# Two closings moved, one routing added: the end of a graph layer with a mixture of experts, replanned

## The chip, the cores and the metric

The kernel runs on one core of a Trainium2 chip. The metric is the device time of one execution in microseconds; three runs are given by their median. The core has five engines with a queue each: PE (matrix products), DVE and ACT (vector and scalar work), POOL (here it does nothing but issue indirect transfers: gathers and scatters of rows by a list of indices) and SP (it issues the plain transfers). Each queue is worked off in order. All transfers share 16 DMA engines.

## The reference

A layer on 6250 nodes of 256 numbers. The nodes are normalised; a graph convolution over 100,000 weighted edges and a linear attention are added; the sum is normalised again and goes through a mixture of 16 experts, of which each node takes two; a last normalisation and the sum are the output.

```python
xn = layernorm(x)
x = x + gnn(xn, edge_index, edge_weight) + mix(xn)       # graph convolution, linear attention
# L0_ffn on layernorm(x):
gate_logits = x @ gate_w + gate_b
topk_vals, topk_idx = top_k(gate_logits, 2)
topk_w = softmax(topk_vals)
h = relu(einsum('bsh,ehf->bsef', x, w1) + b1)            # 16 experts, 256 -> 512
expert_out = einsum('bsef,efh->bseh', h, w2) + b2        # 512 -> 256
y = x + sum over the two (topk_w * their expert_out)
out = old x + (y - mean(y)) / sqrt(var(y) + EPS) * gamma + beta
```

## The kernel before

The nodes lie in 49 tiles of 128 rows. The edges, sorted by their end node, lie in 782 chunks of 128. The kernel is one long hand-written order: a loop over slots, one chunk of edges in each slot, into which pieces of other work are woven. A piece is a generator that is put in at a slot and asks to be called again so many slots later. PE, DVE, ACT and SP execute what the loop writes, in its order. POOL's instructions are not held to that order: a scheduler places them, by what each depends on.

In each slot POOL gathers the 128 source rows of a chunk (`hrow`, L1479), DVE makes a 128 x 128 matrix of edge weights (`hot`, L1484) and PE adds their product into an accumulator (`acc`, L1492). Six to eleven slots lie between the gather of a chunk and its product. When the accumulator of a tile is whole, `residual` makes the tile's new rows, two tiles at a time, and the gate's logits.

After some tiles (`PHASES`, 8, 12, 16 and so on up to 49) a routing follows (`route`, some 70 small instructions on DVE): each of the new tiles' tokens gets two slots in a list of blocks of 128 tokens, each block belonging to one expert. `scatter` then writes the tokens' rows into the slots, two scatters of POOL for each tile (L1144). A block that isn't full stays open, and the next phase's tokens go on filling it. At one phase, the one after `CUT`, the open blocks are closed, so that from there on no token of the tiles below `CUT` stands in a block still to be computed. A closed block may have rows that no token uses.

`expert` computes one block: SP loads its weights (`w1`, `w2` with `b1` and `b2`, 1.15 MB in all) and its rows, PE transposes (L1215) and multiplies them (L1226, L1237), ACT applies the relu (L1233), and SP stores the result (`w_yslots`, issued at L1172). There are always 112 blocks. `hi` says up to which block number each phase's blocks may be begun, `block` at which slots: 7, 6, 5 or 4 slots apart.

`combine` finishes two tiles: POOL gathers each token's two result rows (L1283), DVE adds them, weighted, to the normalised row (L1299, L1301), ACT sums squares (L1306), DVE scales and adds (L1314 to L1320), SP stores the output row (L1321). Which blocks must have been stored before a tile's gather may start is in `LIMITS`: pairs of a tile and a number of blocks. The gather of a tile below 36 waits for block 84, one below 40 for block 99, one below 46 for block 108, the rest for all 112. These bounds depend on the data; `usual` keeps whether they held, and if they didn't, a second pass runs all experts again.

The gathered rows lie in places called `got`: ten rows of `late` and the ten rows of the ring that held the accumulators' sums. A place is taken at the gather and given back after its last reader.

Of the kernel before, what the change touches and what calls it, by code (L numbers as in the profile page):

```python
# [24 lines left out]
F32 = mybir.dt.float32  # L25
# [7 lines left out]
P = 128  # L33
N = 6250
D = 256
# [86 lines left out]

PHASES = (8, 12, 16, 20, 24, 28, 32, 36, 40, 46, NT)
CUT = 36
AFTER = PHASES.index(CUT) + 1
FIRST, USUAL = 2 * PHASES[AFTER] + 5, 2 * NT + 14
LIMITS = ((CUT, FIRST), (PHASES[AFTER], 2 * NT + 2), (PHASES[-2], 2 * NT + 11))
MOST = P  # L130

RING = 10
# [140 lines left out]
def windowed_layer(ctx: ExitStack, tc: tile.TileContext, X, x, ident, loc_t, w_t, src_t, src_r, zero_b, shared, W, b, gamma, beta, wqT, wkvT, wprojT, bproj,  # L273
# [897 lines left out]
    def sync(to, source):  # L1171
        issued[0] = nc.sync.dma_start(to, source).ins  # L1172
        return issued[0]
# [98 lines left out]
    def combine(ts_, homes, pool, last, ahead=9):  # L1272

        n, r = len(ts_), rows(ts_[0])
        total = pool.tile([P, 2], F32, name="total", bufs=3)[:r, :n]
        less = pool.tile([P, 2], F32, name="less", bufs=3)[:r, :n]
        squares = pool.tile([P, 2], F32, name="squares", bufs=3)[:r, :n]
        rs = pool.tile([P, 2], F32, name="rs", bufs=3)[:r, :n]
        got = {}
        for i, t in enumerate(ts_):  # L1280
            for k in range(2):
                got[i, k] = homes["got"].take()
                g = nc.gpsimd.indirect_dma_start(  # L1283
                    out=got[i, k]()[:r], out_offset=None, in_=yslots,
                    in_offset=IndirectOffsetOnAxis(ap=slot_i[:r, t, k:k + 1], axis=0)).ins
                m = next((m for m, (b, _) in enumerate(LIMITS) if t < b), None)
                if m is not None and LIMITS[m][1] - 1 in stores:
                    tc.declare_no_dep(g, group=f"late_{m}", reason="later blocks hold no token of the first tiles")
                    tc.add_manual_dep(g, stores[LIMITS[m][1] - 1].name, mybir.DependencyInfo(mybir.DependencyClass.Sync, mybir.DependencyReason.DATA), reason="the last of their blocks")
                    tc.add_to_no_dep_group(f"gathers_{m}", g)  # L1290
            yield 1
        yield ahead
        both = (pool if pool is not mp_main else xq).tile([P, 2, D], F32, name="xn2", bufs=3)[:r]
        for i, t in enumerate(ts_):
            act(both[:, i, :], X[:r, t, :], AF.Identity, bias=nm2[:r, t:t + 1], scale=rs2[:r, t:t + 1])
        yield 1
        for i, t in enumerate(ts_):
            y = both[:, i, :]
            v.scalar_tensor_tensor(y, got[i, 0]()[:r], w12[:r, t, 0:1], y, op0=OP.mult, op1=OP.add)  # L1299
            homes["got"].give(got[i, 0])  # L1300
            v.scalar_tensor_tensor(y, got[i, 1]()[:r], w12[:r, t, 1:2], y, op0=OP.mult, op1=OP.add,  # L1301
                                   accum_out=total[:, i:i + 1])
            yield 2 if i < n - 1 else 1
        act(less, total, AF.Identity, scale=-1.0 / D)
        for i in range(n):
            act(got[i, 1]()[:r], both[:, i, :], AF.Square, bias=less[:, i:i + 1], accum_out=squares[:, i:i + 1])  # L1306
            homes["got"].give(got[i, 1])
        sd = pool.tile([P, 2], F32, name="sd2", bufs=2)[:r, :n]
        act(sd, squares, AF.Sqrt, bias=eps_t[:r], scale=1.0 / D)
        yield 5  # L1310
        v.reciprocal(rs, sd)
        for i, t in enumerate(ts_):
            y = both[:, i, :]
            v.scalar_tensor_tensor(y, y, less[:, i:i + 1], last[:r, 0, :], op0=OP.add, op1=OP.mult)  # L1314
            o = pool.tile([P, D], F32, name="row", bufs=3)
            if t in shifted:
                v.scalar_tensor_tensor(o[:r], y, rs[:, i:i + 1], shifted[t]()[:r], op0=OP.mult, op1=OP.add)
            else:
                v.scalar_tensor_tensor(y, y, rs[:, i:i + 1], last[:r, 1, :], op0=OP.mult, op1=OP.add)
                v.tensor_add(o[:r], y, X[:r, t, :])  # L1320
            sync(out[t * P:t * P + r, :], o[:r])  # L1321
            yield 2


# [75 lines left out]
    for n, b in enumerate(PHASES):  # L1400
        flush = b == NT
        for t0 in range(a, b, 2):
            t1 = min(b, t0 + 2)
            lag = 3 if t0 < PHASES[AFTER] else 2 if t0 < PHASES[-2] else 1
            at = max(at, evicted_at(min(NCH, 16 * t1 + 4) - 1) - 1)
            weave.add(at, residual(range(t0, t1), lag, 2))
            if t0 >= QT:
                weave.add(at - 8, load_queries(range(t0, t1)))
            last_at = at
            for t in range(t0, t1):  # L1410
                summed_at[t] = at + 3
                if t + RING < NT and t >= 4:
                    sum_from(t + RING)
            at += 10
        hi = 2 * b - (9 if n < AFTER else -1 if n == AFTER else 4)
        ready = max(last_at + residual_slots(lag, 2) + 1, scattered - 2)
        more = min(lag, 3 if n < AFTER else 1)
        def routed(a=a, b=b, lo=lo, hi=hi, n=n, flush=flush, more=more):
            yield from route(a, b, lo, hi, n == 0, n == AFTER, more)
            if flush:  # L1420
                yield 1
                yield from close(hi, USUAL)
        weave.add(ready, routed())
        if flush or n == AFTER:
            weave.add(ready + 6, token_weights(*((CUT, NT) if flush else (0, CUT))))
        slow = 0 if flush else 1
        weave.add(ready + 2, scatter(n, a, b, 8 + more, "token" if slow else "got", slow))
        scattered = ready + 10 + more + 2 * (b - a) * slow
        ready += 13 + more + 2 * (b - a) * slow
        for j in range(lo, USUAL if flush else hi):  # L1430
            ends[j] = hi if j < hi else USUAL
            block = max(block + (4 if n > AFTER or block > NCH - 9 else 5 if n == AFTER else 6 if n == 5 or n == 6 else 7), ready)
            gap = (7, 0) if block < 16 * 30 else (6, 3)
            apart, behind = (5, 3) if block < 16 * 30 else (6, 3) if n < AFTER else (3, 1) if j == USUAL - 1 else (5, 2)
            weave.add(block, expert(n, j, homes, bank, gap, apart, behind, flush))
            stored_at[j] = block + sum(gap) + 2 * apart + behind + 4
        lo, a = hi, b
# [7 lines left out]
        yield  # L1445
    weave.add(last_at + residual_slots(lag, 2) + 1, load_last())
    weave.add(last_at + residual_slots(lag, 2) + 1 + 22, shift(range(NT - 16, NT), last))
    at = last_at + residual_slots(lag, 2) + 1
    for t0 in range(0, NT, 2):
        at = max(at, stored_at[min(block_of(t0), USUAL) - 1])  # L1450
        weave.add(at, combine(range(t0, min(NT, t0 + 2)), homes, mp, last))
# [59 lines left out]
    with tc.If(again[0]), ExitStack() as tail:  # L1511
        tail.enter_context(by_hand(tc))
        mp = tail.enter_context(tc.tile_pool(name="w_again", bufs=2))
        ps = tail.enter_context(tc.tile_pool(name="w_again_ps", bufs=8, space=bass.MemoryType.PSUM))
        last = mp.tile([P, 2, D], F32, name="last", bufs=1)
        nc.sync.dma_start(last[:, 0, :], bcast(f_gamma, D))
        nc.sync.dma_start(last[:, 1, :], bcast(f_beta, D))

        def places(n, size, name):
            tiles = [mp.tile([P, size], F32, name=f"{name}{j}", bufs=1) for j in range(n)]  # L1520
            return Places(*[((), lambda t=t: t) for t in tiles])

        homes = {"x": places(4, D, "x"), "xT": places(2, D, "xT"), "hT": places(2, F, "hT"),
                 "y": places(2, D, "y"), "w1": places(4, WA, "w1"), "w2": places(4, WROW - WA, "w2"), "got": places(8, D, "got")}
        weave = Weave()
        block = 0
        loaded.clear()
        stores.clear()
        shifted.clear()
        row = bank("row")  # L1530
        nc.tensor.matmul(row[0:1, :P], s["code"], ident, start=True, stop=True)
        listed(row, 0, MOST, True)
        for j in range(MOST):
            ends[j] = MOST
            weave.add(block, expert(None, j, homes, bank, (5, 4), 2, 1))
            block += 4
        block += 18
        for t0 in range(0, NT, 2):
            weave.add(block, combine(range(t0, min(NT, t0 + 2)), homes, mp, last, 3))
            block += 6  # L1540
        slot = 0
        while weave.steps:
            weave.run(slot)
            slot += 1
# [485 lines left out]
```

## Time and profile before

| what | value |
|---|---|
| three runs | 1403.89, 1403.41, 1399.54 us (median 1403.41) |
| the profiled execution | 1397.1 us |
| its span in the profile | 1395.2 us |
| mean granted clock of PE | 0.931 |
| PE busy | 1177.9 us, 84% of the span |
| PE's weight loads busy | 983.3 us, 70% |
| POOL busy | 968.4 us, 69% |
| DVE busy | 926.9 us, 66% |
| ACT busy | 523.1 us, 37% |
| moved by DMA | 349 MB, 250 GB/s over the span |

The span is what the profile of one execution covers; the profiled execution's own time is 1.9 us longer, and the median of the three runs lies above both. Busy shares are means over stages of quite different kinds, so they don't name what bounds the kernel; that has to be read stage by stage. POOL's queue holds 752 gathers of edge rows, 98 scatters and 98 gathers of result rows; SP's holds the loads and stores of the blocks and the output.

### The profile page before, as it was taken

How to read it: one execution, taken by the hardware profiler on the slowest of the kernel's cores; microseconds unless marked ns; L12 is line 12 of the kernel's file. 1: busy time of each engine (PE TensorE's matmuls, PEld its weight loads, DVE VectorE, ACT ScalarE, POOL GpSimd, SP SyncE). 2: the span in 40 equal slices, each digit the busy share in tenths (PEclk: the TensorE clock that was granted, in tenths of full speed). 3: DMA queues.
4: the chain of work that ended last, by engine and by line, in shares of the span. 5: the costliest groups of instructions: out<-in, count | busy, mean ns of one | idle time of the engine just before them, and what ended most of it. 6: DMA issues, size and time to landing. Idle time of an engine off the chain costs nothing. (4 is left out here: it accounts for less than half of the span.)

```text
span 1395.2 us, 24302 instructions
## 1 busy us (share of the span) xinstructions
PE 1177.9 (84%) x6908; PEld 983.3 (70%) x6908; DVE 926.9 (66%) x3215; ACT 523.1 (37%) x1476; POOL 968.4 (69%) x1009
## 2 busy tenths in 40 slices
PE   6989999988867589978798699798987998997760
PEld 5757777766656479867687598687876897886650
DVE  8965444457998676847568377485684567646676
ACT  7874444422213123212222132232322233467673
POOL 5637777777777777777777777777777773257753
PEclk9999999998888789989999899898999998999995
DMA  9967667776434658877777788787878987999983
GB/s 299 315 210 247 207 188 228 230 237 191 136 102 128 212 189 279 270 236 252 267 242 252 228 270 286 251 311 247 266 235 284 311 284 239 344 384 383 374 303 97
DMA packets 172870, 349.27 MB, mean 250 GB/s; under 512 B 26460, under 2 KB 112350, under 8 KB 172720
## 3 DMA queue, kind: packets, MB, share of 16 engines
q1 hardware_dynamic: 96376, 189.97, 38.8%
q0 software_dynamic: 47712, 128.17, 29.5%
q10 hardware_dynamic: 28632, 29.40, 6.4%
q8 instruction: 61, 1.00, 0.3%
q14 instruction: 89, 0.73, 0.2%
HBM read 271.62 MB, written 75.81 MB: 249 GB/s over the span
## 5 line engine op out<-in xcount | busy, mean ns | idle before, releaser
L1479 POOL DMA_INDIRECT hrow<-w_hs,src_t x752 | 728.1, 968 | 256.4 <-issue 84.7
L1492 PE MATMUL acc<-hrow,hot 128*128 128x256 f32 x1548 | 429.5, 399 | 75.4 <-DMA hrow<-w_hs,src_t 68.5
L1492 PEld LDWEIGHTS acc<-hrow,hot 128*128 128x128 f32 x1548 | 281.1, 198 | 140.9 <-issue 89.1
L1484 DVE TENSOR_SCALAR hot<-iota_g,loc_t,w_t 128x128 f32<-128x128 f32 x782 | 248.9, 356 | 46.4 <-PE acc L1492 45.1
L1233 ACT ACTIVATE hT<-hp,early 128x128 f32<-128x128 f32 x280 | 79.9, 368 | 234.0 <-PE hp L1226 170.0
L1237 PE MATMUL yp<-early,hT 128*128 128x256 f32 x560 | 138.9, 393 | 0.1
L1226 PE MATMUL hp<-Q,early 128*128 128x128 f32 x944 | 120.1, 282 | 12.1 <-ACT Q L1220 12.1
L1226 PEld LDWEIGHTS hp<-Q,early 128*128 128x128 f32 x944 | 118.1, 199 | 15.3 <-ACT Q L1220 12.8
L1237 PEld LDWEIGHTS yp<-early,hT 128*128 128x128 f32 x560 | 109.6, 199 | 16.5 <-ACT hT L1233 0.8
L1144 POOL DMA_INDIRECT w_xslots<-Q,slot_i x92 | 91.1, 990 | 30.6 <-issue 23.3
L1226 PEld LDWEIGHTS hp<-Q 128*128 128x128 f32 x848 | 104.6, 196 | 2.3
L1226 PE MATMUL hp<-Q 128*128 128x128 f32 x848 | 106.1, 279 | 0.0
L1233 ACT ACTIVATE hT<-hp,Q 128x128 f32<-128x128 f32 x168 | 48.0, 369 | 144.8 <-issue 110.0
L705 PE MATMUL kq<-early,xnT 128*128 128x512 f32 (+1 forms) x196 | 93.7, 601 | 5.2 <-ACT xnT L701 5.2
L713 DVE SCALAR_TENSOR_TENSOR row<-two_a,two_b 128x256 f32<-128x256 f32 (+1 forms) x49 | 20.8, 425 | 96.4 <-ACT two_b L710 96.4
L1237 PE MATMUL yp<-Q,hT 128*128 128x256 f32 x336 | 80.5, 383 | 0.0
L1283 POOL DMA_INDIRECT late<-w_yslots,slot_i x48 | 49.2, 1026 | 39.9 <-issue 22.3
L1237 PEld LDWEIGHTS yp<-Q,hT 128*128 128x128 f32 x336 | 62.8, 192 | 8.0
L350 ACT ACTIVATE sd<-mv,eps_t 128x2 f32<-128x2 f32 (+2 forms) x51 | 15.3, 300 | 127.1 <-DVE mv L346 117.3
L1247 DVE TENSOR_TENSOR Q<-yp,early 128x256 f32<-128x256 f32 x58 | 24.4, 421 | 56.4 <-PE yp L1237 55.8
L709 ACT ACTIVATE two_a<-kq 128x512 f32<-128x512 f32 (+1 forms) x49 | 29.3, 597 | 87.1 <-PE kq L705 66.8
L1215 PE MATMUL xtp<-ident,Q 128*128 128x128 f32 x224 | 43.6, 276 | 20.9 <-DMA Q<-w_xslots 20.6
(374 smaller groups left out, 1941.7 us busy)
## 6 DMA issues: line engine op xcount, KB each, us to landing
early<-in_experts SPq DMA_DIRECT2D x58, 642.0 KB
early<-in_experts SPq DMA_DIRECT2D x59, 512.0 KB
Q<-in_experts SPq DMA_DIRECT2D x53, 512.0 KB
Q<-in_experts SPq DMA_DIRECT2D x30, 642.0 KB
w_yslots<-zero_b ACTq DMA_DIRECT2D x16, 1024.0 KB
Q<-w_xslots SPq DMA_DIRECT2D x112, 128.0 KB
w_yslots<-Q SPq DMA_DIRECT2D x112, 128.0 KB
hrow<-w_hs,src_t POOLq DMA_INDIRECT x752
```

The lines of the kernel that those rows point to most:

```text
L705: nc.tensor.matmul(kq[:r], xnT[:, k, :r], wkq[:, k, :], start=(k == 0), stop=(k == 1))
L709: act(e[:r].rearrange("p a c -> p (a c)"), kq[:r], AF.Exp)
L1144: i = nc.gpsimd.indirect_dma_start(out=xslots, out_offset=IndirectOffsetOnAxis(ap=slot_i[:r, t, k:k + 1], axis=0), in_=y[:r], in_offset=No ...
L1215: nc.tensor.transpose(tp[:, c, :], xs[:, c * P:(c + 1) * P], ident)
L1226: nc.tensor.matmul(hp[:, f, :], w1[:, c, f * P:(f + 1) * P], xT[:, c, :], start=(c == 0), stop=(c == 1))
L1233: act(hT[:, f, :], hp[:, f, :], AF.Relu, bias=b1[:, f:f + 1], scale=1.0)
L1237: nc.tensor.matmul(yp[:, :D], hT[:, f, :], w2[:, f, :], start=(f == 0), stop=(f == FJ - 1 and not as_row))
L1247: v.tensor_add(y, yp[:, :D], b2)
L1283: g = nc.gpsimd.indirect_dma_start(out=got[i, k]()[:r], out_offset=None, in_=yslots, in_offset=IndirectOffsetOnAxis(ap=slot_i[:r, t, k:k + ...
L1479: nc.gpsimd.indirect_dma_start(out=hrows[c], out_offset=None, in_=hs, in_offset=IndirectOffsetOnAxis(ap=src_t[:, c:c + 1], axis=0))
L1484: v.tensor_scalar(hots[c], iota_g[:, group_of(c) % 2, :], loc_t[:, c:c + 1], w_t[:, c:c + 1], op0=OP.is_equal, op1=OP.mult)
L1492: nc.tensor.matmul(accs[g], hots.pop(c), hrows.pop(c), start=begin, stop=end)
```

## The change

The open blocks are closed at the routing after tile 28 (it was 36), a routing at tile 44 is added, and with them the limits, the pace of the blocks and the bounds `hi` are set anew: tiles below 28 wait for block 68, those below 32 for block 97, those below 40 for block 104, those below 46 for block 108. `LATER` is a new name for the phase at 40, from which lags and paces switch as before. The combines begin 13 slots later, counted from the last residual, so that in the written order they stand behind the last scatter. The output row is written into the place of the tile's second gathered row and no longer into one of three rows of its own; the place is given back after the store of the row instead of after ACT's sum of squares. (The second pass gets 14 such places instead of 8.)

```diff
-PHASES = (8, 12, 16, 20, 24, 28, 32, 36, 40, 46, NT)
-CUT = 36
+PHASES = (8, 12, 16, 20, 24, 28, 32, 36, 40, 44, 46, NT)
+CUT = 28
 AFTER = PHASES.index(CUT) + 1
 FIRST, USUAL = 2 * PHASES[AFTER] + 5, 2 * NT + 14
-LIMITS = ((CUT, FIRST), (PHASES[AFTER], 2 * NT + 2), (PHASES[-2], 2 * NT + 11))
+LIMITS = ((CUT, FIRST), (PHASES[AFTER], 2 * NT), (40, 2 * NT + 7), (PHASES[-2], 2 * NT + 11))
+LATER = PHASES.index(40)
...
             act(got[i, 1]()[:r], both[:, i, :], AF.Square, bias=less[:, i:i + 1], accum_out=squares[:, i:i + 1])
-            homes["got"].give(got[i, 1])
...
-            o = pool.tile([P, D], F32, name="row", bufs=3)
+            o = got[i, 1]()
             if t in shifted:
                 v.scalar_tensor_tensor(o[:r], y, rs[:, i:i + 1], shifted[t]()[:r], op0=OP.mult, op1=OP.add)
             else:
                 v.scalar_tensor_tensor(y, y, rs[:, i:i + 1], last[:r, 1, :], op0=OP.mult, op1=OP.add)
                 v.tensor_add(o[:r], y, X[:r, t, :])
             sync(out[t * P:t * P + r, :], o[:r])
+            homes["got"].give(got[i, 1])
...
-            lag = 3 if t0 < PHASES[AFTER] else 2 if t0 < PHASES[-2] else 1
+            lag = 3 if t0 < PHASES[LATER] else 2 if t0 < PHASES[-2] else 1
...
-        hi = 2 * b - (9 if n < AFTER else -1 if n == AFTER else 4)
+        hi = 2 * b - (9 if n < AFTER else 0 if n == AFTER else 5 if b == 44 else 4)
         ready = max(last_at + residual_slots(lag, 2) + 1, scattered - 2)
-        more = min(lag, 3 if n < AFTER else 1)
+        more = min(lag, 3 if n < LATER else 1)
...
-            block = max(block + (4 if n > AFTER or block > NCH - 9 else 5 if n == AFTER else 6 if n == 5 or n == 6 else 7), ready)
+            block = max(block + (4 if n > LATER or block > NCH - 9 else 6 if n > 3 else 7), ready)
             gap = (7, 0) if block < 16 * 30 else (6, 3)
-            apart, behind = (5, 3) if block < 16 * 30 else (6, 3) if n < AFTER else (3, 1) if j == USUAL - 1 else (5, 2)
+            apart, behind = (5, 3) if block < 16 * 30 else (6, 3) if n < LATER else (3, 1) if j == USUAL - 1 else (5, 2)
...
-    at = last_at + residual_slots(lag, 2) + 1
+    at = last_at + residual_slots(lag, 2) + 14
     for t0 in range(0, NT, 2):
         at = max(at, stored_at[min(block_of(t0), USUAL) - 1])
         weave.add(at, combine(range(t0, min(NT, t0 + 2)), homes, mp, last))
         at += 5
```

The rule of the limits itself is unchanged: a combine gather waits for the store of the last block in its tile's limit, and the stores of later blocks are declared to be no concern of it.

More of the change, by code (lines that the diff above doesn't have):

```diff
@@ L1523, in windowed_layer @@
         homes = {"x": places(4, D, "x"), "xT": places(2, D, "xT"), "hT": places(2, F, "hT"),
-                 "y": places(2, D, "y"), "w1": places(4, WA, "w1"), "w2": places(4, WROW - WA, "w2"), "got": places(8, D, "got")}
+                 "y": places(2, D, "y"), "w1": places(4, WA, "w1"), "w2": places(4, WROW - WA, "w2"), "got": places(14, D, "got")}
         weave = Weave()
```

## The prediction

> **What bounds the kernel now.** I read the busy lines first, then windows of 10 us across the end, then POOL's and SP's timelines, then the waits from 1150 us on.
>
> ```profile
> 1148.44 0.98 POOL L1479 DMA_INDIRECT hrow<-w_hs,src_t  x1 [0.30 <-PE acc L1492]
> 1149.72 0.95 POOL L1479 DMA_INDIRECT hrow<-w_hs,src_t  x1 [0.30 <-PE yp L1237]
> 1153.52 1.00 POOL L1144 DMA_INDIRECT w_xslots<-Q,slot_i  x1 [2.85 <-issue]
> ...
> 1206.96 0.97 POOL L1144 DMA_INDIRECT w_xslots<-late,slot_i  x1 [38.24 <-DVE d L1058]
> ...
> 1213.94 1.56 POOL L1144 DMA_INDIRECT w_xslots<-late,slot_i  x1 [0.30 <-issue]
> 1232.61 0.99 POOL L1283 DMA_INDIRECT late<-w_yslots,slot_i  x1 [17.11 <-issue]
> ...
> 1348.77 0.94 POOL L1283 DMA_INDIRECT late<-w_yslots,slot_i  x1 [8.81 <-DVE xn L1319]
> ...
> 1372.20 1.56 POOL L1283 DMA_INDIRECT late<-w_yslots,slot_i  x1 [0.30 <-DVE row L1317]
> ```
>
> POOL (start, duration, and in brackets the idle time before) issues one indirect transfer per 0.95 + 0.30 = 1.25 us, and the windows give it 38 of every 50 us from 150 to 1150: up to 1149.72 the kernel runs at POOL's pace, with PE, DVE and DMA below it. The end is another stage: the last edge gather at 1149.72, twelve scatters, 38 us for the last routing, six scatters, 17 us idle, then 98 combine gathers in one run (73 of them before 1328.53) with one stop of 8.8 us ahead of tile 40.
>
> ```profile
> 1170.00:1180.00 10.00, 9.49 (x65) 8.72 (x64) 9.49 (x29) 4.26 (x15) 0.00 (x0) 1.00 0.67 212
> 1190.00:1200.00 10.00, 10.00 (x70) 9.24 (x70) 4.67 (x21) 6.43 (x18) 0.00 (x0) 1.00 0.89 278
> 1210.00:1220.00 10.00, 10.00 (x65) 8.51 (x63) 8.01 (x35) 4.17 (x14) 4.59 (x4) 1.00 1.05 403
> 1290.00:1300.00 10.00, 7.82 (x53) 6.75 (x53) 4.94 (x15) 6.54 (x22) 7.57 (x9) 1.00 1.03 387
> 1330.00:1340.00 10.00, 8.52 (x59) 7.22 (x58) 7.15 (x21) 7.79 (x27) 6.42 (x7) 1.00 1.05 401
> 1370.00:1380.00 10.00, 0.00 (x0) 0.00 (x0) 8.31 (x25) 6.76 (x23) 3.28 (x2) 0.50 0.31 92
> ```
>
> Columns: PE, PEld, DVE, ACT, POOL busy, granted clock, DMA share, GB/s. To 1200 PE is full and DMA is not; from 1200 to 1340 DMA is full (share 1.00 to 1.05; the ten windows from 1200 to 1300 average 387 GB/s) and PE falls to 6.6 to 8.5 of 10; from 1350 DVE alone works, on the last combines.
>
> ```profile
> 1131.31 0.36 SPq L1172 DMA_DIRECT2D w_yslots<-Q  x1
> 1226.42 0.36 SPq L1172 DMA_DIRECT2D w_yslots<-Q  x1
> 1328.53 0.36 SPq L1172 DMA_DIRECT2D w_yslots<-Q  x1
> 1346.23 0.35 SPq L1172 DMA_DIRECT2D w_yslots<-Q  x1
> ```
>
> ```profile
> DVE row L1320 <- DMA out_dram<-row: 28.6, 16, 3.3
> PE xtp L1215 <- DMA Q<-w_xslots: 20.1, 17, 2.2
> SPq L1172 <- DVE row L1320: 4.1, 4, 2.3
> ```
>
> Counted back from the last store (block 111, at 1354.94) these four stores are of blocks 68, 84, 104 and 108. Block 84 releases the first combine 6.2 us later (1232.61), block 108 tile 40 (1348.77). In the waits from 1150 on, PE's only large one is for token rows behind full DMA engines, DVE's for the three output rows.
>
> **The change, part by part.** Slots are the loop's own count; I worked both schedules out from its arithmetic.
>
> *Earlier closing, even pace.* There are still 112 blocks, so no PE work is added or removed. Blocks 47 to 75 move up, by 16 slots at most and 2 from block 75 on. When PE takes the last edge product (slot 787, 1171.87 now) it has the second product of 73 blocks behind it and not 72: -4.1 us, a block's period in the PE timeline (1224.28 to 1228.30), where PE is the limit. The counts of tokens per expert that follow from the reference's inputs fit every new limit (112 of 112 blocks at the end), so the second pass over all experts isn't taken.
>
> *Routing at tile 44.* One routing costs DVE about 16 us (the lines of routing sum to 182 us for eleven). It lies at slots 741 to 760, in 1100 to 1150, where DVE is busy 31.2 of 50 us: 47 of 50 with it. Hidden, at 0; without that cover hots come late and PE pays up to 16. I take 0.
>
> *POOL's order.* Built, the changed program has the eight scatters of tiles 40 to 43 ahead of the last 13 edge gathers, and seven combine gathers among these 13. The seven wait for block 68, stored 10 slots (12 us) sooner than 1131.31; POOL gets there at about 1147, so they don't stop it. The last edge gather goes out 15 issues x 1.27 = 19 us later, at 1169; with some 6 us to land and be multiplied (3.8 to 7.0 in the chain of waits) PE is through at 1175, not 1171.87: +3.5. Behind it stand residual and routing of tile 48 and the last six scatters. With the -4.1 above: -0.6 (from -4 if POOL's delay is covered to +8 if DVE's 16 us show too).
>
> *Combines begun early.* Seven gathers before the last edge gathers and ten before the last six scatters, 17 in all, leave the full stretch for one in which DMA has room. Up to block 104's store the full stretch carried 73 gathers and 23 output rows (POOL's and SP's timelines). Now tiles 32 on wait for that block, so it carries 64 - 17 = 47 gathers and some 30 rows: 26 - 7 = 19 transfers fewer, of 131 KB or 0.34 us at 387 GB/s each: -6.5 us. By time rather than bytes the bounds are 0 and -6.5.
>
> The Trainium skill ("Perfetto Trace Analysis", Identifying the Most-Contended Engine) warns that occupancy of the 16 DMA engines misleads and that one should look at HBM utilization, and "DMA: Bandwidth & Descriptors", Where 436 GB/s comes from, says that some 358 GB/s of HBM per core bind. By that rule share 1.05 proves nothing, and the term could be 0. The 403 GB/s of this trace are above 358, so that limit isn't what holds here; 436 from the same section would leave 8% free and make it -5.7.
>
> *Output rows in gather places.* DVE's 28.6 us of waits go, since twenty places replace three rows. What hides most of it is DMA: PE waits for rows that full engines bring. On the path lies at least what SP, which also issues the blocks' loads, loses behind these rows (4.1 us); at most PE's whole 20.1. I take -2, half of SP's, and 0 and -20 for the range. A place now comes back only after its row has left. Twenty places hold ten tiles, at 2.7 us per tile 27 us; a place is needed for some 5 us of gathering, 2 of landing, 8 to the final DVE step and 6 to leave, 21. I count nothing, and carry the far side in the slower case: a gather that waits for a row to leave holds POOL's whole queue, then DVE's pass for that pair, then ACT, which stands behind DVE with the blocks' hT. On SP the stores of output rows now stand among the loads of blocks 85 to 104 instead of 88 to 108, at the same two per five slots: nothing.
>
> *What ends last.* Block 104 is stored at 1328.5 - 0.6 - 6.5 - 2 = 1319.4. Behind it now stand 34 gathers (tiles 32 to 48), not 18 behind block 108. First gather 6.2 later, as after block 84; 34 x 1.34 (1232.61 to 1338.87 in 79 steps) = 45.6; then 8.8 (2.5 to land, 1.5 for the pair before, 4.8 for the last tile, 1380.51 to 1385.3): 1380.0. Now the last DVE step ends at 1385.3. The other chain, seven DVE passes of 4.15 after the last block, moves with that block by -9 and ends before it. So -5.3.
>
> **Sum.** The profiled execution took 1397.1 (span 1395.2 and 1.9 around it): 1391.8. The median of the runs is 6.3 above that execution: 1398.1. I say 1398.
>
> **The rivals.**
>
> *Slower: 34 gathers behind one store.* POOL's queue is in order, and tiles 32 to 35, which needed block 84, now need 104. From that store to the end it is 6.2 + 45.6 + 8.8 = 60.6 us, so if it lands in time later than 1324.7 the kernel is slower. If bytes aren't the limit, 1328.5 stays; with the +3.5 of the late edge gathers and the 1.39 per gather of the last stretch (+1.7) the end is 1394.3, +9.0: 1412. For it: the stop ahead of tile 40 shows that POOL does wait for blocks, and DMA was a quarter to a third free at 1150 to 1180 (shares 0.73, 0.76, 0.67) without help to PE. Against: share 1.0 through 1328.
>
> *No change: 1403.* Bytes leave the full stretch and come back as idle engines in the two pauses that the limits at 98 and 105 blocks force on POOL; the order of ACT and DVE behind the last block (seven passes) is the same as before. For it: that order. Against: the pauses let PE run at 4.1 us a block where it now takes 5.3.
>
> *Much faster.* The output rows held SP and with it PE: PE's 20.1 us go, 1397.1 - 20 + 6.3 = 1383. For it: the 28.6 us. Against: DMA at its peak.
>
> **How the numbers follow.** Forecast 0.50, slower 0.28, no change 0.11, much faster 0.11. About 0.3% (4.2 us) is what a measurement here tells from nothing. The forecast's own range is 1390 to 1402; a fifth of it (0.10) lies within 0.3%. So faster 0.40 + 0.11 = 0.51, same 0.10 + 0.11 = 0.21, slower 0.28. The range 1385 to 1411 reaches into the much faster and the slower case.
>
> **What would show it.** Right: POOL's last L1480 at about 1169 with combine gathers before it; 17 gathers before the last scatter at 1215; block 104's store near 1320; DVE's wait for output rows gone; POOL idle twice before tiles 28 and 32. Wrong: block 104 after 1325, POOL stopped at its first combine gather, or gathers waiting for output rows to leave.

## The result: slower by 0.8%, and the profile after

| | before | changed |
|---|---|---|
| median of five runs | 1400.42 us | 1411.84 us |
| lowest to highest | 1398.51 to 1403.89 | 1409.86 to 1414.22 |
| span of the profiled execution | 1395.2 us | 1409.9 us |
| last edge product begins on PE | 1171.87 | 1184.15 |
| block 104 stored | 1328.53 | 1340.78 |
| combine gathers behind the store that POOL waits for last | 18 (block 108, 1346.23) | 34 (block 104) |
| last DVE operation ends | 1385.3 | 1400.3 |

The ratio is 1.0082, 95% interval 1.0066 to 1.0098: slower by 11.4 us, where 2 us faster than this median (5.3 faster in the trace) was forecast. The time also lies 0.8 us above the stated range.

The trace shows two places. The first is POOL's timeline of the changed kernel (start, duration, in brackets the idle time before):

```profile
1144.83 0.97 POOL L1145 DMA_INDIRECT w_xslots<-Q,slot_i  x1 [0.30 <-DMA Q<-in_experts]
1146.11 0.98 POOL L1480 DMA_INDIRECT hrow<-w_hs,src_t  x1 [0.30 <-PE xtp L1216]
...
1157.74 0.95 POOL L1284 DMA_INDIRECT src_r<-w_yslots,slot_i  x1 [0.30 <-issue]
1158.99 0.94 POOL L1480 DMA_INDIRECT hrow<-w_hs,src_t  x1 [0.30 <-PE yp L1238]
...
1163.18 0.94 POOL L1284 DMA_INDIRECT agg<-w_yslots,slot_i  x1 [0.30 <-issue]
1164.43 0.94 POOL L1480 DMA_INDIRECT hrow<-w_hs,src_t  x1 [0.30 <-PE acc L1493]
...
1170.66 0.94 POOL L1480 DMA_INDIRECT hrow<-w_hs,src_t  x1 [0.30 <-issue]
...
1228.30 1.56 POOL L1145 DMA_INDIRECT w_xslots<-late,slot_i  x1 [0.30 <-issue]
...
1345.57 0.94 POOL L1284 DMA_INDIRECT late<-w_yslots,slot_i  x1 [21.95 <-DMA w_yslots<-Q]
...
1389.70 1.76 POOL L1284 DMA_INDIRECT src_r<-w_yslots,slot_i  x1 [0.30 <-DMA src_r<-w_yslots,slot_i]
```

Eight scatters end at 1145.8. Then the last 13 edge gathers go out with seven combine gathers among them, the last edge gather at 1170.66. PE's timeline around the same rows:

```profile
1151.84 1.22 PE L1493 MATMUL acc<-hrow,hot 128*128 128x256 f32 x2 [4.85 <-DMA hrow<-w_hs,src_t]
...
1171.11 1.22 PE L1493 MATMUL acc<-hrow,hot 128*128 128x256 f32 x2 [6.42 <-DMA hrow<-w_hs,src_t]
...
1184.15 0.59 PE L1493 MATMUL acc<-hrow,hot 128*128 128x256 f32 x2
```

Windows of 10 us (PE, PEld, DVE, ACT, POOL busy, granted clock, DMA share, GB/s):

```profile
1150.00:1160.00 10.00, 7.35 (x18) 5.03 (x19) 7.04 (x31) 0.00 (x0) 7.80 (x8) 0.53 0.52 168
1160.00:1170.00 10.00, 4.34 (x31) 3.28 (x29) 4.39 (x24) 2.00 (x6) 7.63 (x8) 0.98 0.74 236
1170.00:1180.00 10.00, 8.16 (x31) 6.46 (x32) 1.09 (x2) 0.59 (x1) 7.18 (x8) 0.68 0.49 174
1340.00:1350.00 10.00, 9.31 (x64) 8.13 (x65) 0.00 (x0) 4.33 (x14) 3.51 (x4) 1.00 1.01 366
```

PE stands still before the first row behind the eight scatters (4.85 us) and before the first behind the combine gathers (6.42 us), and what it does next runs at half the clock: a pair of products takes 1.22 us where it takes 0.59 at 1184.15. All such waits from 1140 to 1186 add up in one line of the waits (us, times, longest):

```profile
PE acc L1493 <- DMA hrow<-w_hs,src_t: 13.2, 6, 6.4
```

Before, the same stretch had no wait for edge rows. The Trainium skill ("TensorE: Matmul & The Clock Gate", What's actually happening) says that PE falls to half its clock after an idle window of some 3.4 us; the gaps of 4.85 and 6.42 us followed by 0.53 and 0.68 agree with it. But the kernel before loses its clock in this stretch too, and its longest gap there is 1.97 us. Its PE timeline and its window:

```profile
1154.88 0.47 PE L803 MATMUL tp<-ident,shared 128*128 128x128 f32 x2 [1.97 <-DVE shared L1501]
...
1157.66 1.22 PE L1492 MATMUL acc<-hrow,hot 128*128 128x256 f32 x2
```

```profile
1150.00:1160.00 10.00, 6.87 (x33) 4.21 (x31) 9.42 (x36) 0.47 (x1) 5.62 (x7) 0.76 0.73 224
```

Its granted clock is 0.73 from 1160 to 1170. An estimate: added up over the PE rows that take longer here than the same operations do at full clock, the half clock costs some 4.5 us before and some 5.8 us in the changed kernel, up to the last edge product. The clock is a small part of the difference, the waits are the large one.

The second place is the end. SP issues block 104's store at

```profile
1340.78 0.36 SPq L1173 DMA_DIRECT2D w_yslots<-Q  x1
```

and POOL, which had waited 21.95 us for it, begins its last 34 gathers 4.8 us later. DVE has nothing to do from 1340 to 1350 (0.00 in the window above; 7.44 before).

### The profile page after: what moved, and what is told of

Same layout as the page of the kernel before. It is cut to its first block, busy times and chain, and to the rows that moved or that the text cites. A ratio compares the mean times of both kernels' runs of the same rounds, so it can differ in the third digit from the quotient of the medians.

```text
span 1409.9 us, 24317 instructions
## 1 busy us (share of the span) xinstructions
PE 1183.3 (84%) x6914; PEld 987.8 (70%) x6914; DVE 936.0 (66%) x3290; ACT 523.8 (37%) x1476; POOL 971.4 (69%) x1009
## 5 line engine op out<-in xcount | busy, mean ns | idle before, releaser
L1227 PE MATMUL hp<-Q,early 128*128 128x128 f32 x944 | 122.4, 286 | 14.1 <-ACT Q L1221 13.3
L706 PEld LDWEIGHTS kq<-early,xnT 128*128 128x128 f32 (+1 forms) x196 | 37.0, 190 | 32.0 <-issue 23.8
```

Of the source, the lines that this page charges most:

```text
L706: nc.tensor.matmul(kq[:r], xnT[:, k, :r], wkq[:, k, :], start=(k == 0), stop=(k == 1))
L1227: nc.tensor.matmul(hp[:, f, :], w1[:, c, f * P:(f + 1) * P], xT[:, c, :], start=(c == 0), stop=(c == 1))
```

## The experiments

Theory A: the loss comes from POOL's order around the last edge gathers, and block 104's store sets the end. Theory B: the limits and full DMA set the end whatever happens earlier. Theory C: gathers wait for output rows to leave their places. All times below are differences from the kernel before, run beside each on the same chip; ratios come with their 95% interval.

Eleven of the eighteen runs fell on three chips (numbered 6, 7 and 10) where the kernel before takes 1642 to 1648 us, called the slower chips below. The other seven fell on two chips (3 and 4) where it takes 1400 us. In the run on a slower chip with output rows of their own, PE's waits ahead of edge products from 1330 to 1420, where the edges end, are 2.8 us and none of them is put down to edge rows; on chip 3 the same kernel has 14.0 us of these. So those runs say little of the question; the seven on chips 3 and 4 decide. Moments read from traces are those of one execution each, and executions of one kernel spread by some us (1398.2 to 1405.6 with the gathers held, on chip 3): a difference of 2 or 3 us between two traces is weak evidence.

**The combine gathers behind the edges.** A dependence without a semaphore from each combine gather on the last edge gather, which fixes only the order on POOL's queue:

```diff
-            nc.gpsimd.indirect_dma_start(
+            last_edge[0] = nc.gpsimd.indirect_dma_start(
                 out=hrows[c], out_offset=None, in_=hs,
...
+                tc.add_manual_dep(g, last_edge[0].name, mybir.DependencyInfo(mybir.DependencyClass.NoSync, mybir.DependencyReason.DATA), reason="behind the edges")
```

> The changed kernel with one thing different: each combine gather stands behind the last edge gather on POOL, so the seven gathers that stood among the last 13 edge gathers come after them. Theory A (POOL's order): PE's waits of 6.4, 0.7 and 0.35 us for edge rows that came behind those seven go, the last edge product moves from 1184.4 to about 1177, block 104's store from 1340.8 to about 1334, and the end with it: 4 us slower than before in place of 11.4. Theory B (limits and full DMA): what is won at 1180 is lost in the full stretch, block 104 stays within 2 us of 1340.8, 11 us slower than before. Theory C (places): nothing changes, 11 us slower.

On a slower chip: 1.0074 (1.0042 to 1.0105).

> The changed kernel with each combine gather behind the last edge gather, once more, because before took 1648 us beside its first run, on a chip where neither POOL nor the end had the times of the profile that was read. Where before takes about 1400: theory A (POOL's order) expects the last edge product at about 1177, block 104's store at about 1334 and 4 us slower than before; theory B (limits and full DMA) the store within 2 us of 1340.8 and 11 us slower.

1402.26 against 1400.49 us, ratio 1.0008 (0.9988 to 1.0029): no longer to be told from before, and better than the 4 us slower that theory A expected. Against the changed kernel that is 9.6 us by the medians (11.4 less 1.8), or 0.0074 by the ratios, with some 0.0026 (3.6 us) either way. POOL's timeline:

```profile
1145.71 0.97 POOL L1145 DMA_INDIRECT w_xslots<-Q,slot_i  x1 [0.30 <-issue]
...
1162.42 0.95 POOL L1482 DMA_INDIRECT hrow<-w_hs,src_t  x1 [0.30 <-PE xtp L1217]
1163.67 0.94 POOL L1285 DMA_INDIRECT shared<-w_yslots,slot_i  x1 [0.30 <-issue]
...
1336.06 0.94 POOL L1285 DMA_INDIRECT late<-w_yslots,slot_i  x1 [24.37 <-DMA w_yslots<-Q]
...
1380.21 1.81 POOL L1285 DMA_INDIRECT src_r<-w_yslots,slot_i  x1 [0.30 <-DMA src_r<-w_yslots,slot_i]
```

The last edge gather goes out 8.2 us sooner, and PE's waits from 1140 to 1186 are now

```profile
PE acc L1495 <- DMA hrow<-w_hs,src_t: 5.0, 1, 5.0
```

The wait behind the eight scatters stays, the others go; the last product begins at 1173.69 (10.5 sooner), block 104 is stored at

```profile
1330.22 0.36 SPq L1173 DMA_DIRECT2D w_yslots<-Q  x1
```

10.6 sooner, and the last DVE operation ends 9.6 sooner. A gain at 1170 comes through whole to the end: that excludes B for this part, and C.

**Without the routing at 44.** `PHASES` loses its 44; first alone, then with the gathers held as above.

> The changed kernel without the routing at tile 44; the first seven combine gathers still stand among the last edge gathers, the eight scatters of tiles 40 to 43 behind them. Theory A: PE's waits behind those eight scatters (4.85, 0.3 and 0.5 us) go and those behind the seven gathers stay: last edge product at about 1179, end 5 us earlier than the changed kernel's: 6 us slower than before. Theory B: 11 us slower. Theory C: 11 us slower.

On a slower chip: 1.0069 (1.0041 to 1.0098).

> The changed kernel without the routing at tile 44 and with each combine gather behind the last edge gather: POOL's order is that of before up to the last edge gather, all else is as changed. Theory A: PE waits for no edge row, the last edge product is at 1169 to 1173, block 104 is stored at 1320 to 1325, and 60.6 us lie behind it: 0 to 5 us faster than before. Theory B: what is won is lost again in the full stretch, block 104 comes at 1335 or later, 7 us slower or more.

1.0092 (1.0063 to 1.0121), 13.1 us slower: theory A missed. PE's waits for edge rows do shrink, to 1.7 us, but PE waits 8.1 us for ACT's hT in their place, and the last edge product begins at 1178.74. ACT's timeline shows why hT is late:

```profile
1166.27 0.60 ACT L1134 ACTIVATE Q<-X,nm,rs 128x256 f32<-128x256 f32 x1 [20.07 <-DMA w_xslots<-Q,slot_i]
```

ACT takes its work in order too and stood 20.07 us at an operation that waits for a scatter; hT comes behind it. In this run the seven held gathers stand between the last edge gather and the scatters, the first of which goes out at 1162.41 (1153.52 before, where ACT waited 11.78 us). So the seven seem to cost here as well, by another way; that was not tested by itself. SP's stores show blocks 75 and 76 at

```profile
1190.60 0.35 SPq L1173 DMA_DIRECT2D w_yslots<-Q  x1
1206.29 0.35 SPq L1173 DMA_DIRECT2D w_yslots<-Q  x1
```

15.7 us apart, against 4.6 with the routing (1187.55, 1192.15). With the closing at 28, `hi` lets only blocks up to 75 begin before the next routing (80 before the change). Without the routing at 44 that next one is at 46, and block 104 comes at 1341.54. So the routing at 44 belongs to the earlier closing, as it is written here. What it costs by itself is small: without it block 69 was stored at 1129.70, with it at 1133.32.

**Output rows.** Back in three rows of their own in the changed kernel (and the gather's place given back as before), and in gather places in the kernel before (there with the combines begun 13 slots later, as these need it):

```diff
-            o = got[i, 1]()
+            o = pool.tile([P, D], F32, name="row", bufs=3)
```

> The changed kernel with output rows in three rows of their own again. Theory C (places): POOL's waits for output rows to leave (17 us in five stops between 1280 and 1314) go and most of it is gained: 1 to 5 us slower than before in place of 11.4. Theory A: those stops are covered by the wait for block 104 that follows; DVE's waits for rows return, and the time stays or grows by 2: 11 to 14 us slower than before. Theory B: 11 us slower.

On a slower chip: 1.0117 (1.0074 to 1.0159).

> The changed kernel with output rows in three rows of their own, once more for the same reason. Theory C (places): 1 to 5 us slower than before. Theories A and B: 11 to 14 us slower, DVE waiting for rows again.

1.0093 (1.0063 to 1.0124), 13.7 us slower; the changed kernel had 1.0082. The difference of 0.0011, some 1.5 us, is smaller than either interval: the rows' worth can't be told from nothing. DVE's wait is back, as the waits from 1235 to 1370 show:

```profile
DVE row L1321 <- DMA out_dram<-row: 24.5, 17, 2.9
```

Most of it was hidden, since the time hardly moved. C is out: nothing was gained.

> The kernel before with the output rows in gather places alone (and, as these need it, the combines begun 13 slots later in the written order; POOL's order stays that of before). Theory A and the prediction's term: 2 us faster than before (0 to 5). Theory C: gathers wait for rows to leave and the kernel is 5 us slower or more. Theory B: no change.

> The kernel before with the output rows in gather places alone, once more, because before took 1648 us beside its first run. Taking the rows back out of the changed kernel cost 2.4 us; by theory A they are worth the same here: 2 us faster than before (0 to 5). Theory C: 5 us slower or more.

> The kernel before with the output rows in gather places alone, on a chip where before takes about 1400 us. By the prediction's term 2 us faster (0 to 20); by the 2.4 us that their return cost in the changed kernel, 2.4 us faster; by theory C (gathers wait for rows to leave) 5 us slower or more.

All three on slower chips: 1.0012 (0.9983 to 1.0041), 0.9996 (0.9954 to 1.0037), 1.0010 (0.9977 to 1.0043). No change is seen there, but each interval is too wide to exclude 2 us faster or C's 5 us slower; on chips 3 and 4 it wasn't measured.

**Closing and limits alone.** The changed kernel without the routing at 44, with rows of their own, combines begun as before:

> The kernel before with the earlier closing, its limits, pace and bounds alone (no routing at 44, rows of their own, combines begun as before); POOL's order has seven combine gathers ahead of the last eight edge gathers, and twelve scatters behind them. Theory A: PE waits some 7 us for edge rows, and 34 gathers stand behind block 104: 5 to 9 us slower than before. Theory B: 9 to 13 us slower. Theory C: no slower than before.

1.0134 (1.0094 to 1.0174), 19.2 us slower, more than any theory said: block 76 waits for the routing at 46 here too (1206.65), PE waits 7.1 us for hT as without the routing at 44 above, and block 80 is 25.5 us behind the kernel before. Theory A had not seen these waits.

**What sets the end.** With the gathers held, the limits at two blocks fewer (these inputs need 103 blocks for the tiles below 40 and 107 for those below 46, so that nothing is to spare):

```diff
-LIMITS = ((CUT, FIRST), (PHASES[AFTER], 2 * NT), (40, 2 * NT + 7), (PHASES[-2], 2 * NT + 11))
+LIMITS = ((CUT, FIRST), (PHASES[AFTER], 2 * NT), (40, 2 * NT + 5), (PHASES[-2], 2 * NT + 9))
```

> The changed kernel with the combine gathers behind the last edge gather and two limits set to what the routing of these inputs needs: tiles below 40 wait for block 102 instead of 104, tiles below 46 for block 106 instead of 108. Theory A with its end (the last stretch is the 34 gathers that POOL may not issue before one store): in the run with the gathers held, block 102 was stored 8.2 us before block 104, so the end comes 8 us earlier than there: 6 us faster than before (3 to 9). Theory B (full DMA engines and the order of DVE and ACT behind the last block set the end): the earlier gathers only take bandwidth from the blocks: 0 to 2 us slower than before, as with the gathers held alone.

On a slower chip: 1.0069 (1.0033 to 1.0106).

> The changed kernel with the combine gathers behind the last edge gather and the two limits set to what the routing of these inputs needs, once more, for a chip where before takes about 1400 us. If the 34 gathers behind block 104 set the end: 6 us faster than before (3 to 9). If full DMA engines and the order of DVE and ACT behind the last block set it: 0 to 2 us slower.

1394.31 against 1400.45 us, 0.9963 (0.9946 to 0.9980): 6.1 us faster than before, the only version here that beats both kernels. Block 102 was stored at 1325.09, and POOL's last stop and last gather are

```profile
1329.98 0.95 POOL L1285 DMA_INDIRECT late<-w_yslots,slot_i  x1 [14.09 <-DVE xn L1321]
...
1374.68 1.60 POOL L1285 DMA_INDIRECT src_r<-w_yslots,slot_i  x1 [0.30 <-DVE xn L1316]
```

The 34 gathers begin 6.1 us sooner than in the run with the gathers held and end 5.5 sooner, although block 104 itself came 3.0 later. So what releases them sets the end, and the limit moved it. That this is the store itself is the likely reading: the first gather comes 4.9 us behind block 102's store, where the changed kernel has 4.8 and the run with the gathers held 5.8 behind block 104's. The trace names a DVE operation as the last releaser here, though, and the edit does two things at once: in the written order the combines of tiles 32 on also move forward by 8 slots, on DVE and ACT too; which of both counts was not separated.

The same edit on the kernel before (blocks 98 and 105):

> The kernel before with its two later limits set to what the routing of these inputs needs there: tiles below 40 wait for block 98 instead of 99, tiles below 46 for block 105 instead of 108. POOL's stop of 8.8 us ahead of tile 40 goes, since block 105 was stored at 1333.67. If the stop sets the end, the last gather and the end come up to 8 us earlier; if the seven DVE passes behind the last block (4.15 us each from 1355 on) set it, some of them move ahead of the last block and it is 2 to 5 us faster; theory B expects no change.

On a slower chip: 0.9988 (0.9953 to 1.0023).

> The kernel before with its two later limits at blocks 98 and 105, once more. If POOL's stop of 8.8 us ahead of tile 40 sets the end: up to 8 us faster. If the DVE passes behind the last block do: 2 to 5 us faster. If full DMA does: no change.

0.9994 (0.9972 to 1.0015), no change. POOL's stop of 8.8 us is gone and its last gather comes 4.0 us sooner, yet the last DVE operation does not. POOL's timeline:

```profile
1368.24 1.56 POOL L1283 DMA_INDIRECT late<-w_yslots,slot_i  x1 [0.30 <-DVE row L1317]
```

DVE's:

```profile
1385.29 0.48 DVE L1317 SCALAR_TENSOR_TENSOR row<-xn,rs,Q 106x256 f32<-106x256 f32 x1 [0.28 <-DMA out_dram<-row]
```

So POOL's stop did not set the end before the change. The likely reading is that the end belongs to the DVE passes behind the last block, whose place in the written order this edit leaves alone (the combines follow each other by 5 slots there, later than any limit). The 2 to 5 us expected from passes that move ahead of the last block did not come: none moved. "No change" is also what the full DMA engines were to give, and this run does not part the two.

**No gather early.** All 17 early gathers also behind the last scatter:

> The changed kernel with all combine gathers behind the last edge gather and behind the last scatter, so that none of the 17 early ones leaves the full stretch. By the prediction's term (0.34 us of full DMA for each transfer) block 104 is stored 17 x 0.34 = 5.8 us later than in the run with the gathers held behind the edges alone (1330.2), at 1336, and the kernel is 7 us slower than before. If bytes are not what holds the blocks: block 104 at 1330 or earlier, since DVE and ACT have no combines beside the last routing: 0 to 2 us slower.

On a slower chip: 1.0105 (1.0044 to 1.0166).

> The changed kernel with all combine gathers behind the last edge gather and the last scatter, once more. By 0.34 us of full DMA for each of the 17 transfers: block 104 at 1336, 7 us slower than before. If bytes are not what holds the blocks: block 104 at 1330 or earlier, 0 to 2 us slower.

1.0031 (1.0016 to 1.0046), 3.7 us slower; block 104 at 1332.45. Moving 17 transfers out of the full stretch is worth 2.2 us at block 104 against the run with the gathers held, or 0.13 us each; counted from block 74 on it is 4.1 us, or 0.24 each. Both are below 0.34 and lie between both expectations, but they compare one execution on chip 4 with one on chip 3, and the intervals of the two ratios overlap.

**The eight scatters.** Edge gathers written 15 slots earlier, and each scatter of tiles 40 to 43 tied behind the edge gather written last, so that they alternate; with the gathers held, and once more with the lower limits too:

> The changed kernel with the combine gathers behind the last edge gather, the last edge gathers written 15 slots earlier, and each scatter of tiles 40 to 43 behind the edge gather written last before it, so that eight scatters and edge gathers alternate on POOL instead of eight scatters going first. Theory A: PE's waits of 6.2 us behind the eight scatters shrink to 3 or less, block 104 comes 3 us earlier than with the gathers held alone (1327), and the time is 1 to 4 us less than there: 0 to 3 us faster than before. If those waits are covered by something else: as with the gathers held alone, 0 to 2 us slower than before.

> The same with the two limits at blocks 102 and 106. Theory A: both gains add, 7 to 10 us faster than before. If the waits behind the scatters are covered: 6 us faster, as with the gathers held and these limits.

Both on a slower chip: 1.0033 (1.0006 to 1.0061) and 1.0064 (1.0031 to 1.0097). They settle nothing; what the 5.0 us behind the scatters cost on chips 3 and 4 stays open.

## Why the prediction was wrong

*POOL's order: the step that failed.* The order itself was right (last edge gather forecast at 1169, measured 1170.66; seven gathers among the last 13, seventeen before the last scatter). What failed is "some 6 us to land and be multiplied, PE is through at 1175: +3.5". That looks at the last gather alone. PE takes its work in the written order, so it stands still before every late row, not only the last, and the blocks' products that lie between the last six edge products cannot be done meanwhile: they still stood behind the wait that ended at 1171.11, and took until 1184.15. Forecast for the last edge product: +3.5; measured: +12.3. With the block done earlier the blocks were to be 0.6 us ahead behind the edges; block 74 was 6.6 late. Holding the seven gathers back returned 10.5 of the 12.3, and some 10 us of the time: this is shown, and it is most of the loss of 11.4.

*Earlier closing, -4.1.* Right: with the gathers held, block 74 was stored at 1180.59 against 1184.50, 3.9 sooner.

*Routing at 44, taken as 0.* About right as a cost (3.6 us at block 69, caught up by block 75). That blocks 76 on can't begin without it before the routing at 46 was not in the prediction.

*Bytes and rows, -6.5 and -2: the second step that failed.* Not found. Behind the edges block 74 is 6.6 us late and block 104 12.2: the stretch lost 5.6 us where it was to gain 8.5. Block 104 was forecast 9.1 sooner and came 12.2 later; of these 21.3 us, 7.2 lie ahead of block 74 and 14.1 in this stretch, so the larger part of the miss is here, though the loss against the kernel before comes mostly from POOL's order. Inside it, blocks 74 to 92 lose 13.3 and blocks 92 to 104 win back 7.7. The run with the gathers held has the same 5.6 (-3.9 to +1.7), and the run without early gathers 9.7 (-5.8 to +3.9), so the early gathers do not look like the cause; their worth looks positive, but smaller than 0.34 us each. In that stretch DVE is busy 72.99 of 99 us (55.92 of 91 before), and PE's waits for token rows are 5.8 us (2.0 before) and for DVE and ACT 6.2 (0.7 before); which of these brings it stays open.

*Places returned late, 0.* Right as far as the runs show: five stops of POOL for rows to leave, 17 us in all and the longest 11.1 before 1313.61, lie ahead of the stop for block 104, which ends at 1345.57 anyway; with rows of their own block 104 came no sooner (1343.80).

*From block 104 to the end, 60.6 us.* Right: 59.5 (4.8 to the first gather for 6.2, 45.9 for the 34 gathers for 45.6, 8.8 behind them for 8.8).

*The slower rival* named the mechanism (34 gathers behind block 104, decisive from 1324.7 on) and 1412 us. It came within 0.2 us, partly by chance: it put that store at 1332, not 1340.8, and took the median 6.3 us above the profiled execution, while here the two agree. The no-change rival expected idle engines in the pauses that the limits force on POOL. DVE is idle at 1340 to 1350, but the DMA engines are not: their share is 1.04, 0.98 and 1.01 in the three windows from 1320 to 1350.

## What to carry to other kernels

When transfers are moved ahead of others on an in-order issuing queue, walk through the consumer's order and add up its wait at every late row: the landing of the last one gives only a lower bound. A limit that lets most tiles start early helps only if what waits for the later limit is short: count the work behind the last release and carry it to the end. And look at what an earlier closing makes the next routing responsible for, before calling that routing a cost or a saving.

## What the runs showed that was not expected

PE's stall of 4.85 us left it at half clock (1.22 us for a pair of products that takes 0.59), so a short gap cost more than its length; and the kernel before ran at half clock behind gaps of 1.97 us at most. One and the same kernel took 1400 us on two chips and 1642 to 1648 on three others. Those traces show 136 or 137 instructions on POOL from 600 to 800 instead of 157 to 159 and, in the kernel before with rows in gather places, 54.5 us of POOL's waits (32 of them, 300 to 1100) ended by a release that the trace calls remote, of which the profile of the kernel before at 1397 us shows none. Why the chips differ stays open. A version's standing differs between them: the changed kernel with the gathers held gave 1.0074 on chip 7 and 1.0008 on chip 3.
